# First loads, spectral norms, due steps and last outputs of a two-layer attention kernel

## The chip, the cores and the metric

The kernel runs on one core of a Trainium2 chip. A core has TensorE (PE, matrix products), VectorE (DVE), ScalarE (ACT), GpSimd (POOL) and SyncE (SP); each takes its instructions strictly in its own order, and they wait for each other by semaphores. Transfers between the memory and the core's buffers are issued by SP, ACT and POOL. The metric is the device time of one execution in microseconds (us), as the median of several runs. A profiled execution gives the busy times and waits below; its span runs from the first to the last instruction.

## The reference

The input x is 8 images of 64 x 64 pixels with 256 channels, in float32. Two layers follow each other.

Layer 0: `qkv = x @ w_qkv` gives queries and keys; the values are the keys. The first 128 channels attend in horizontal windows (8 rows of 64 pixels, 4 heads of 32 channels), the other 128 in vertical windows (8 columns). Beside this a depthwise 3x3 convolution runs over `hard_swish(v)`; then `context = hard_swish(attention + convolution)` and `x = context @ w_out + b_out`.

Layer 1: three small projections f, g, h (32 channels each) and one back to 256 channels, each weight divided by its spectral norm (`w / sigma`, one power step from a given vector u). All 4096 pixels of an image attend to all: `softmax(g f^T) h`, projected with `wv`, times gamma, plus x.

## The kernel before

Each image is a chain of units: 8 horizontal windows (h0 to h7, 4 steps each), 8 vertical windows (v0 to v7, 3 steps each) and 2 global units (l0, l1, 32 steps each); h0 of the next image stands ahead of l0. A step is a block of scores on TensorE (four heads as 32-row products, L777, L801, L1016), two exps on ScalarE into a ring of eight weight slots (L560), and a block of values products for the step before (L823, L830, L1032). VectorE adds up the weights for the softmax sums (L839, L847, L854, L1047); in the global units POOL's DMAs add up one of four head rows (L1056, L1058).

Everything else is a task that a planner, class `Flow`, fits between the steps while the program is built: projections of x in four quarters of two 256-column pieces (`project`, L306; m = 0 and 2 are the "near" queries and keys for the horizontal windows, m = 1 and 3 the "far" ones for the vertical windows), convolution taps (`conv`, eight on VectorE, L708), joins, clips and contexts, sums and norms, the layer-1 projections (`project_fg`, `project_h`), and the results (`result`). A task has a due step, made from the table `DUE` and the unit's own step, and pieces with estimated costs (`ADD`, `TAPS`, ...). `fill_pe`, `fill_act` and `fill_dve` take the ready task that is due first, as far as the planner's own clocks say that it fits; `require` runs a task at once when a step needs it. So a change of `DUE` or of a cost changes the order of instructions on every engine.

Ahead of the planned part, the program loads the weights (L351 to L392) and works out the spectral norms (L404 to L452): VectorE multiplies and reduces, three products on TensorE (L424, L425) sum over partitions, ScalarE takes a square root (L443). The first image's first load of x is issued on SP behind these loads (`load`, L617). A single bank of PSUM (`mm_tile`) serves projections, sums and norms in turn, so the next of them waits until the last is copied out. Keys reach the values products by a chain: eviction on ScalarE (L649), transpose on VectorE (L718), a DMA to memory (L723), four DMAs back (L734).

The end is written out by hand: `last_blocks` multiplies contexts by `w_out` and `last_ends` adds the global part (L1119), evicts with ScalarE (L1125) into two buffers `ot` and stores (L1129); `limits` checks the range of the softmax sums and sets a flag by a small product (L470). A flag out of range would start an exact second version of the kernel, which doesn't run with these inputs.

## Time and profile before

| | |
|---|---|
| median of 3 runs | 3292.57 us (3291.46 to 3293.92) |
| the profiled execution | 3294.1 us, span 3292.3 us |
| TensorE busy | 3244.5 us, 99% of the span |
| VectorE busy | 2666.3 us, 81% |
| ScalarE busy | 2667.3 us, 81% |
| GpSimd busy | 513.4 us, 16% |
| granted TensorE clock, mean | 0.996 |
| read from and written to HBM | 99.78 MB and 83.89 MB |

The profile names engines as PE (products), PEld (weight loads, which overlap PE), DVE, ACT, POOL and SP; PEq, ACTq and SPq are the sequencers that issue. L306 is line 306 of the kernel. In rows of groups and of the timeline, `out<-in` are the program's names of tiles, `32*128 32x512` the shape of weights and of what is streamed, `x8` how many instructions (one float32 product is two), and in brackets the idle time of the engine before them and what ended it. Matmuls are pipelined and their ends modelled, so start times tell more than ends.

### The profile page before, as it was taken

How to read it: one execution, taken by the hardware profiler on the slowest of the kernel's cores; microseconds unless marked ns; L12 is line 12 of the kernel's file. 1: busy time of each engine (PE TensorE's matmuls, PEld its weight loads, DVE VectorE, ACT ScalarE, POOL GpSimd, SP SyncE). 2: the span in 40 equal slices, each digit the busy share in tenths (PEclk: the TensorE clock that was granted, in tenths of full speed). 3: DMA queues.
4: the chain of work that ended last, by engine and by line, in shares of the span. 5: the costliest groups of instructions: out<-in, count | busy, mean ns of one | idle time of the engine just before them, and what ended most of it. 6: DMA issues, size and time to landing. Idle time of an engine off the chain costs nothing. (4 is left out here: it accounts for less than half of the span.)

```text
span 3292.3 us, 83473 instructions
## 1 busy us (share of the span) xinstructions
PE 3244.5 (99%) x35348; PEld 1191.2 (36%) x35348; DVE 2666.3 (81%) x2404; ACT 2667.3 (81%) x3235; POOL 513.4 (16%) x776
## 2 busy tenths in 40 slices
PE   7999999999999999999999999999999999999998
PEld 3344233432335323353233433334333443334422
DVE  4898688986989869897689976899768997789874
ACT  5778888887888878888788887888877888778785
POOL 0001320012200222002210032100321003210132
PEclk9999999999999999999999999999999999999999
DMA  2125653356433564335643365423753236632465
GB/s 73 58 85 118 126 105 100 88 116 132 105 92 91 114 134 97 94 95 115 132 97 91 95 126 125 97 86 98 135 120 98 81 106 127 125 94 69 108 123 108
DMA packets 321117, 344.40 MB, mean 105 GB/s; under 512 B 34272, under 2 KB 198624, under 8 KB 320736
## 3 DMA queue, kind: packets, MB, share of 16 engines
q0 software_dynamic: 71680, 134.25, 23.1%
q1 hardware_dynamic: 246816, 204.18, 21.0%
q8 instruction: 280, 4.59, 0.6%
q10 hardware_dynamic: 2240, 0.56, 0.1%
q14 instruction: 101, 0.83, 0.1%
HBM read 99.78 MB, written 83.89 MB: 56 GB/s over the span
## 5 line engine op out<-in xcount | busy, mean ns | idle before, releaser
L560 ACT ACTIVATE p<-s 128x1024 f32<-128x1024 f32 x1664 | 1612.2, 1024 | 195.3 <-PE s L1016 113.9
L1047 DVE TENSOR_TENSOR acc_l<-acc_l,p 128x1536 f32<-128x1536 f32 x480 | 842.7, 1756 | 312.1 <-ACT p L560 308.1
L708 DVE SCALAR_TENSOR_TENSOR act<-hv,dw_sb,act 128x1024 f32<-128x1024 f32 x512 | 653.5, 1280 | 15.2 <-ACT act L704 4.3
L1016 PE MATMUL s<-gq,f 32*128 32x512 f32 x4096 | 618.3, 641 | 1.7 <-DMA gq<-fg 1.7
L1032 PE MATMUL num_l<-p,h_sb 128*32 128x512 f32 x4096 | 545.4, 604 | 0.3 <-ACT nums_l L1062 0.3
L306 PE MATMUL pq<-x,wqkv_sb 128*32 128x256 f32 x8192 | 516.1, 381 | 4.4 <-ACT kv L653 2.1
L306 PEld LDWEIGHTS pq<-x,wqkv_sb 128*32 128x32 f32 x8192 | 265.2, 110 | 349.5 <-issue 191.3
L1016 PEld LDWEIGHTS s<-gq,f 32*128 32x128 f32 x4096 | 187.1, 183 | 332.4 <-issue 323.7
L801 PE MATMUL s<-qh,kh 32*128 32x512 f32 x2048 | 296.2, 640 | 6.5 <-ACT qh L634 5.7
L1058 POOL DMA_DIRECT2D row_l<-p x240 | 210.8, 878 | 522.5 <-ACT p L560 467.6
L1058 POOL DMA_DIRECT2D acc_l<-p x240 | 210.5, 877 | 426.7 <-ACT p L560 332.3
L830 PE MATMUL num_h<-p,vs 128*32 128x512 f32 x2048 | 272.8, 605 | 2.9 <-DMA vs<-kvia 2.7
L306 PE MATMUL s<-act,wout_sb 128*32 128x512 f32 x2048 | 227.6, 594 | 0.2 <-ACT ot_l L1125 0.2
L1032 PEld LDWEIGHTS num_l<-p,h_sb 128*32 128x32 f32 x4096 | 80.9, 108 | 383.8 <-issue 371.3
L777 PE MATMUL s<-qv,kv 32*128 32x256 f32 x3072 | 213.8, 394 | 1.4 <-ACT p L560 1.4
L1098 ACT ACTIVATE ot_l<-s,bias_o 128x512 f32<-128x512 f32 x120 | 76.0, 685 | 152.6 <-PE s L306 144.2
L823 PE MATMUL num_v<-p,vs 128*32 128x256 f32 x3072 | 193.6, 385 | 0.0
L839 DVE TENSOR_TENSOR acc_h<-p 128x2048 f32<-128x2048 f32 x64 | 146.3, 2285 | 53.5 <-PE sum_h L869 48.0
L1056 POOL DMA_DIRECT2D acc_l<-p x16 | 9.2, 577 | 1145.0 <-PE sum_h L869 961.5
L777 PEld LDWEIGHTS s<-qv,kv 32*128 32x128 f32 x3072 | 144.2, 184 | 78.4 <-issue 52.9
L839 DVE TENSOR_TENSOR acc_v<-p 128x2048 f32<-128x2048 f32 x64 | 146.6, 2291 | 21.0 <-PE sum_h L869 9.8
L790 ACT ACTIVATE p<-s 128x1024 f32<-128x1024 f32 x128 | 131.4, 1027 | 27.0 <-PE s L777 27.0
(140 smaller groups left out, 3214.6 us busy)
## 6 DMA issues: line engine op xcount, KB each, us to landing
acc_l<-p POOLq DMA_DIRECT2D x256, 256.0 KB, 3.3
row_l<-p POOLq DMA_DIRECT2D x256, 256.0 KB, 3.4
x<-in_xT SPq DMA_DIRECT2D x92, 512.0 KB, 4.1
kvia<-kt SPq DMA_DIRECT2D x128, 256.0 KB, 2.4
vs<-kvia SPq DMA_DIRECT2D x512, 64.0 KB, 2.1
out<-ot_l SPq DMA_DIRECT2D x128, 256.0 KB, 2.1
via_v<-nums_v SPq DMA_DIRECT2D x64, 256.0 KB, 2.1
shuf_v<-via_v SPq DMA_DIRECT2D x256, 64.0 KB, 2.1
```

What stands on the lines that cost most here:

```text
L306: nc.tensor.matmul(out[quad(r), :], lhsT=lhsT[:, quad(r)], rhs=rhs, start=start, stop=stop)
L560: nc.scalar.activation(pt[:, 2 * z : 2 * z + 2, :], sc[z], AF.Exp, scale=scale)
L708: nc.vector.scalar_tensor_tensor(o, src, wt, o, ALU.mult, ALU.add)
L777: mm = nc.tensor.matmul(place_of(n, r, h, sc), lhsT=k[quad(r), t * P : (t + 1) * P], rhs=q[quad(r), side(h)], start=True, stop=True,)
L801: nc.tensor.matmul(row_of(sc, r), lhsT=k[quad(r), c * P : (c + 1) * P], rhs=q[quad(r), :], start=True, stop=not exact,)
L823: nc.tensor.matmul(u["num"][quad(r), side(h)], lhsT=vs[kind, i][:, r, t, :], rhs=place_of(n, r, h, (pt[:, :2], u["mid", c], pt[:, 2:])), s ...
L830: nc.tensor.matmul(u["num"][quad(r), :], lhsT=vs[kind, i][:, r, c, :], rhs=u[c][:, r, :], start=(c == 0), stop=(c == 3),)
L839: nc.vector.tensor_add(u["acc"], u["acc"] if c == 2 else u[0], u[c])
L1016: nc.tensor.matmul(row_of(sc, r), lhsT=f4[quad(r), c * P : (c + 1) * P], rhs=gq[quad(r), z, :], start=True, stop=not exact,)
L1032: nc.tensor.matmul(u["num"][quad(r), :], lhsT=h_sb[:, c, :], rhs=u[c][:, r, :], start=(c == 0), stop=(c == 4 * NB - 1),)
L1047: nc.vector.tensor_add(acc, u[0][:, :rows, :] if c == 1 else acc, u[c][:, :rows, :])
L1058: nc.gpsimd.dma_start(out=u["row", c % 2], in_=u[c][:, rows, :], accum_op=ALU.add)
```

## The change

- The key half of `w_qkv` is loaded first on SP, then the first block of x, then the query half. `b_qkv` moves to ScalarE's queue; `dw`, `wv` (four copies), gamma and the small biases move from SP and ScalarE to POOL's queue.
- The spectral norms become four planner tasks (`scale`, `spread`, `norms`, `divide`) that run among the first image's steps, with their scratch in `f4`, which the first image needs only later. The square root is made on VectorE by four Newton rounds from an integer start value; ScalarE runs one dummy exp early.
- The planner charges 0.12 more for a VectorE task that depends on the one before it, with lower costs otherwise, and may take another ready task instead if that one's due step is at most `other` steps later (a value that can be negative).
- Due steps of their own for the first image (`first_...`), for each block's projections (`ahead`, `k`, `q`), swishes and joins, for the vertical windows' sums, release, norm and context, and for the results; all of the table has new values. Keys are required before queries at a window's start.
- The last unit's outputs go to eight slots of the weight ring in place of two buffers, and VectorE evicts every second of them; the last sums stand between two blocks of products.

Cut to its core, the diff is:

```diff
@@ DUE and costs
-    near_k=-7, near_q=-2, near_values=-50, clip=42, swish=21, conv_h0=106, conv_h1=18, conv_h2=27,
-    conv_h3=36, conv_v0=65, conv_v1=13, conv_v2=32, conv_v3=27, tap=-21, join_h=-53, join_hl=28,
-    join_v=12, context=-28, norm=14, release=-34, sums=-18, add=48, adds_h=1, adds_v=0, group_h=0,
-    group_v=1, add2=12, add3=98, apart=8, fg0=-7, fg2=-15, fg3=3, h0=36, h1=7, values_v=-102, near0=-69,
-    spread0=14, spread1=66, spread_mid=68, conv_first=80, far_swish=-20,
+    ahead1=104, ahead2=7, ahead3=1, ahead4=17, k0=-13, k1=52, k2=-18, k3=0, k4=-3, k5=18, k6=-3, k7=7,
+    q0=70, q1=31, q2=-14, q3=-2, q4=70, q5=4, q6=0, q7=99, join_h0=38, join_h1=17, join_h2=23,
+    join_h3=23, join_h4=-12, join_h5=26, join_h6=-17, join_h7=58, join_v0=26, join_v1=19, join_v2=20,
+    join_v3=-25, join_v4=-148, join_v5=-22, join_v6=22, join_v7=-5, swish1=98, swish2=-48, swish3=-133,
+    swish4=17, far_swish0=101, far_swish1=5, far_swish2=-23, far_swish3=28, far_swish4=46,
+    far_swish5=-127, far_swish6=3, far_swish7=-2, result0=121, result1=-27, release_v=-9, norm_v=11,
+    sums_v=-54, context_v=-34, clip_v=70, other=-91, first_ready=42, first_near=-1, first_k=1,
+    first_q=-2, first_swish_v=-3, first_swish_h=54, first_conv_h=6, first_conv_v=22, near_k=-4,
+    near_q=91, near_values=-10, clip=141, swish=12, conv_h0=168, conv_h1=16, conv_h2=24, conv_h3=39,
+    conv_v0=17, conv_v1=23, conv_v2=29, conv_v3=69, tap=-21, join_h=-73, join_hl=24, join_v=1,
+    context=-43, norm=18, release=-7, sums=66, add=26, adds_h=1, adds_v=0, group_h=0, group_v=1,
+    add2=-44, add3=93, apart=6, fg0=-7, fg2=31, fg3=120, h0=32, h1=12, values_v=-74, near0=-55,
+    spread0=4, spread1=72, spread_mid=61, conv_first=309, far_swish=-2,
 )
...
-ADD, ADD3, NORM, SWISH, TAP, TAPS = 2.36, 1.83, 2.5, 0.75, 0.75, 1.28
+ADD, ADD3, NORM, SWISH, TAP, TAPS, BOUND = 2.21, 1.68, 2.39, 0.61, 0.61, 1.2, 0.12
...
@@ Flow
+                if engine == "dve":
+                    took += BOUND * self.bound(task)
+                    self.dve_last = task
...
+    def bound(self, task):
+
+        return task is self.dve_last or self.dve_last in task.needs
+
...
-                self.run(min(ready, key=lambda k: k.due))
+                best = min(ready, key=lambda k: k.due)
+                if self.bound(best):
+                    others = [k for k in ready if not self.bound(k) and k.due <= best.due + DUE["other"]]
+                    best = min(others, key=lambda k: k.due, default=best)
+                self.run(best)
...
@@ first loads
+    three_e = const.tile([P, 1], F32, name="three_e")
 
     wqkv_sb = const.tile([P, 2, 2 * C], F32, name="wqkv_sb")
-    nc.sync.dma_start(out=wqkv_sb, in_=w_qkv.rearrange("(k p) m -> p k m", p=P))
+    wq = w_qkv.rearrange("(k p) m -> p k m", p=P)
+    nc.sync.dma_start(out=wqkv_sb[:, :, C:], in_=wq[:, :, C:])
+    later = [lambda: nc.sync.dma_start(out=wqkv_sb[:, :, :C], in_=wq[:, :, :C])]
     bqkv_sb = const.tile([P, 4], F32, name="bqkv_sb")
-    nc.sync.dma_start(out=bqkv_sb, in_=b_qkv)
+    nc.scalar.dma_start(out=bqkv_sb, in_=b_qkv)
     h_sb = const.tile([P, N // P, D], F32, name="h_sb")
     raw = h_sb[:, : 2 * 3, :].rearrange("p (k z) d -> p k z d", k=2)
...
-    u_r = rows(ufgh.rearrange("z o d -> o (z d)"), 3 * D, "u_r")
-    wv_raw = prep.tile([P, C], F32, name="wv_raw")
-    for r in range(NQ):
-        nc.sync.dma_start(out=wv_raw[quad(r), :], in_=wv)
-    uv_r = rows(uv, C, "uv_r")
-    gam = rows(gamma, 1, "gam")
...
-    pb = mm_tile("norms")
-    for k in range(2):
-        nc.tensor.matmul(pb[:, :NF], lhsT=ones, rhs=ext[:, k, :], start=(k == 0), stop=(k == 1))
-    nc.tensor.matmul(
-        pb[:, NF : NF + C + 1], lhsT=ones[:D, :], rhs=ext_v[:D, :], start=True, stop=True
-    )
-    sums = prep.tile([P, NF + C + 1], F32, name="sums")
...
-    nc.scalar.activation(inv, inv, AF.Sqrt)
...
+    def spectral(scratch):
...
+        u_r = rows(ufgh.rearrange("z o d -> o (z d)"), 3 * D, nc.scalar)
+        uv_r = rows(uv, C, nc.scalar)
+        nc.scalar.dma_start(out=wout_sb, in_=w_out.rearrange("(k p) m -> p k m", p=P))
+        nc.gpsimd.dma_start(out=dw_sb, in_=dw)
+        nc.gpsimd.dma_start(out=dwb_sb, in_=dw_bias)
+        wv_raw = part(C)
+        for r in range(NQ):
+            nc.gpsimd.dma_start(out=wv_raw[quad(r), :], in_=wv)
+        gam = rows(gamma, 1, nc.gpsimd)
+        nc.gpsimd.dma_start(out=bout_c, in_=b_out)
+        nc.gpsimd.dma_start(out=b_raw, in_=bfgh)
+        bv_c = part(2)
+        nc.gpsimd.dma_start(out=bv_c, in_=bv)
...
+        def scale():
+            nc.vector.tensor_scalar_mul(wout_sb, wout_sb, 1.0 / 6.0)
+            nc.vector.tensor_scalar_mul(dw_sb, dw_sb, 1.0 / 6.0)
+
+        def spread():
...
+        def norms():
+            pb = mm_tile("norms")
+            for k in range(2):
+                nc.tensor.matmul(
+                    pb[:, :NF], lhsT=ones, rhs=ext[:, k, :], start=(k == 0), stop=(k == 1)
+                )
+            nc.tensor.matmul(
+                pb[:, NF : NF + C + 1], lhsT=ones[:D, :], rhs=ext_v[:D, :], start=True, stop=True
+            )
+            nc.vector.tensor_copy(sums, pb[:, : NF + C + 1])
+        def divide():
...
+            nc.vector.tensor_scalar(
+                root.bitcast(I32), inv.bitcast(I32), -0.5, float(0x5F3759DF), ALU.mult, ALU.add
+            )
+            for _ in range(4):
+                nc.vector.tensor_mul(t, root, root)
+                nc.vector.tensor_mul(t, t, inv)
+                nc.vector.tensor_scalar(t, t, -0.5, 1.5, ALU.mult, ALU.add)
+                nc.vector.tensor_mul(root, root, t)
+            nc.vector.tensor_mul(inv, inv, root)
...
+        return scale, spread, norms, divide
...
@@ load
+                while later:
+                    later.pop()()
...
@@ last_blocks, last_ends
-                    if js[0] == 0:
-                        u["po", m] = []
-                    pair = pairs.popleft()
-                    pairs.append(pair)
-                    for i, j in enumerate(js):
-                        u["po", m].append(pair[:, i, :])
+                    for j in js:
+                        if j % 2 == 0:
+                            pair = pairs.popleft()
+                            pairs.append(pair)
+                            u["po", m] = [*u.get(("po", m), ()), pair[:, 0, :], pair[:, 1, :]]
...
-                        ot = work.tile([P, TB], F32, tag="ot", name=f"ot_{nm}_{j}_{m}", bufs=out_bufs)
-                        nc.scalar.activation(
-                            ot, u["po", m][j], AF.Identity, bias=bias_o[:, m : m + 1]
-                        )
+                        ot = weights_at(4 * m + j, 1)[:, 0, :]
+                        if j % 2:
+                            nc.vector.tensor_scalar_add(ot, u["po", m][j], bias_o[:, m : m + 1])
+                        else:
+                            nc.scalar.activation(
+                                ot, u["po", m][j], AF.Identity, bias=bias_o[:, m : m + 1]
+                            )
...
@@ the norms as tasks
-        combined = []
+        combined, scaled = [], []
         if not exact:
+            scale, spread, norms, divide = spectral(f4)
+            nc.scalar.activation(three_e, three, AF.Exp)
+            scaled.append(flow.add("dve", [(scale, [("dve", NORM)])], 6, ready=1))
+            k = flow.add("dve", [(spread, [("dve", NORM)])], 7, ready=1)
+            k = flow.add("pe", [(norms, [("pe", 1.5), ("dve", TAP)])], 10, [k], ready=3, bank=True)
+            k = flow.add("dve", [(divide, [("dve", 5.5)])], 14, [k], ready=4)
             combined.append(
-                flow.add("pe", [(combined_weights, [("pe", 5.0), ("dve", NORM)])], 24, ready=16, bank=True)
+                flow.add(
+                    "pe", [(combined_weights, [("pe", 5.0), ("dve", NORM)])], 24, [k, *scaled], ready=16,
+                    bank=True,
+                )
             )
...
@@ due steps
+                total.then = (last, e + DUE["sums" if u.kind != "v" else "sums_v"])
...
+            u.released = flow.add("act", [(u.release, [("act", COPY)])], e + DUE["release" if u.kind != "v" else "release_v"], ready=e)
...
+                due = start + inside_due(i, 0) + DUE[f"ahead{i}"] if inside else None
...
+                    ready, due = (start, start + inside_due(i, 1) + DUE[f"{'kq'[m == 1]}{i}"]) if last else (0, u.t + DUE["first_k" if m == 3 else "first_q"])
...
+                        due = start + inside_due(i, 1) + DUE["far_swish"] + DUE[f"far_swish{i}"] if last else u.t + DUE["first_swish_v"]
...
+                        due += 0 if last else DUE["first_conv_v" if half else "first_conv_h"]
...
+                    due += DUE[f"join_{'hv'[kind]}{i}"]
...
-                    u.ends.append(flow.add("res", pieces, u.t + u.steps + 4 * m, [u.normed], im.ends[-1:]))
+                    u.ends.append(flow.add("res", pieces, u.t + u.steps + DUE[f"result{m}"], [u.normed], im.ends[-1:]))
-                h[i].ahead = {0: [near[i, 0], near[i, 2]]}
+                h[i].ahead = {0: [near[i, 2], near[i, 0]]}
...
...
@@ the end
-                u.last_blocks(0, (2, 3))
+                u.last_blocks(0, (2,))
                 flow.require(u.total, u.released)
+                u.last_blocks(0, (3,))
                 u.last_blocks(1, (0, 1))
                 flow.require(u.normed)
```

## The prediction

> **What bounds the kernel now.** I read the page first: TensorE is busy for 99% of the span, VectorE and ScalarE for 81% each.
>
> ```profile
> PE 3244.5 (99%) x35348; PEld 1191.2 (36%) x35348; DVE 2666.3 (81%) x2404; ACT 2667.3 (81%) x3235; POOL 513.4 (16%) x776
> PE   7999999999999999999999999999999999999998
> ```
>
> So only what makes TensorE wait, or stretches a row of it, can be won. Second, the busy times by stretch (columns: stretch and length, then busy time and instructions of PE, PEld, DVE, ACT, POOL, then clock, DMA share, GB/s): the first 40 us, a slow stretch, the vertical windows of the second image, and the end.
>
> ```profile
> 0.00:20.00 20.00, 7.80 (x70) 3.75 (x70) 6.48 (x27) 2.68 (x4) 1.59 (x16) 1.00 0.33 87
> 26.70:33.40 6.70, 5.79 (x44) 2.56 (x48) 2.89 (x2) 1.54 (x3) 0.00 (x0) 0.50 0.02 5
> 585.00:684.00 99.00, 99.00 (x1340) 48.84 (x1340) 91.85 (x97) 85.69 (x105) 0.00 (x0) 1.00 0.31 89
> 3258.00:3292.00 34.00, 21.72 (x180) 6.03 (x176) 7.64 (x15) 8.86 (x13) 1.74 (x2) 0.87 0.31 88
> ```
>
> TensorE does nothing useful for 12.2 of the first 20 us and 12.3 of the last 34; from 26.7 to 33.4 its clock is half; and in the vertical windows VectorE is at 93%, next in line to bound.
>
> Third, the timeline, which shows what a step costs. First the global stage without a filler, then a step with one quarter of a projection.
>
> ```profile
> 721.72 1.31 PE L1016 MATMUL s<-gq,f 32*128 32x512 f32 x8
> 723.96 1.14 PE L1016 MATMUL s<-gq,f 32*128 32x512 f32 x8
> 726.02 1.34 PE L1016 MATMUL s<-gq,f 32*128 32x512 f32 x8
> ...
> 803.68 1.14 PE L1016 MATMUL s<-gq,f 32*128 32x512 f32 x8
> 805.63 0.61 PE L306 MATMUL pq<-x,wqkv_sb 128*32 128x256 f32 x8
> 806.18 1.14 PE L1016 MATMUL s<-gq,f 32*128 32x512 f32 x8
> ```
>
> Starts of scores: plain steps take 2.24 and 2.06 in turn (the odd one waits for an exp to free a bank), the one with a quarter 2.50. Sorting all 512 global steps of the trace by content: plain 2.154 on average with 2.066 the least, one quarter 2.50, two 2.93, four 3.79, that is 2.066 + 0.43 per quarter. A filled step hides what the exps cost; a plain one after a plain one loses.
>
> Last, timeline and chain rows at the start, at the last image's global stage, and at the end.
>
> ```profile
> 7.11 0.40 SPq L617 DMA_DIRECT2D x<-in_xT  x1
> 13.17 3.51 PE L306 MATMUL pq<-x,wqkv_sb 128*32 128x256 f32 x32 [0.71 <-DVE sums L429]
> 27.61 1.94 PE L830 MATMUL num_h<-p,vs 128*32 128x512 f32 x8 [2.66 <-DMA vs<-kvia]
> 178.79 1.07 PE L830 MATMUL num_v<-p,vs 128*32 128x512 f32 x8 [3.12 <-DMA vs<-kvia]
> 190.11 1.07 PE L869 MATMUL sum_v<-acc_v,ones 128*32 128x256 f32 x16 [1.79 <-DVE acc_v L854]
> 3092.07 2.04 PE L1016 MATMUL s<-gq,f 32*128 32x512 f32 x2 [1.73 <-DMA gq<-fg]
> 3281.76 1.28 ACT L1125 ACTIVATE ot_l<-s,bias_o 128x512 f32<-128x512 f32 x2 [2.68 <-PEq L1562]
> 3285.39 1.28 ACT L1125 ACTIVATE ot_l<-s,bias_o 128x512 f32<-128x512 f32 x2 [2.35 <-DMA out<-ot_l]
> ```
>
> The first projection starts at 13.17, behind the norms on TensorE; each of the next four rows is a wait of TensorE; the last evictions wait for output buffers.
>
> **The change part by part.** Gains are against the profiled execution: 3294.1, of which 3292.3 is span; it lies 1.5 above the median 3292.57, so I take the same gain off the median.
>
> *Start.* The first image load moves from seventh to second on SP's queue: SP's second issue stood at 1.26, so it leaves 5.85 earlier than 7.11. The page's median landing of such a load is 4.1, which gives 5.4; wqkv's halves land beside it, so I take 6.2. The norms no longer stand ahead on TensorE, so the first projection gains 13.17 - 6.2 = 7.0. Bounds: 7.8 (landing as the median); 4.0 if 1.0 MB must pass first at the 131 GB/s of the best 100 us (7.9 us, start at 9.2). The wv, gamma and bias loads go to POOL's queue, ten issues at about 0.88 (the POOL rows), all out before 11, and the halo memsets behind them aren't needed until about 20. ScalarE keeps seven issues and loads the exp table before there is anything to evict; the two loads of 1.28 (at 9.57 and 21.45) become one.
>
> *First values.* Keys are projected before queries. From the end of the key eviction to the first values product the trace has 20.19 to 27.61, 7.4. In the new order TensorE fills this with 0.05 + query projection 1.93 + 0.82 to its eviction's end, scores 1.07, projection 1.75, scores 0.95 = 6.6, so about 0.8 of the 2.66 stays: 1.9 won. The clock fell to 0.50 from 26.7 to 33.5 after this gap, 6.8 us at half, 3.4 lost; gaps of 0.8 elsewhere leave it at 1.00, so I count the 3.4 too: 5.3 (1.9 to 6.0). The next image load now waits on SP behind the value fetches (issue near 16, landed near 20.5; its projection comes near 22.5).
>
> *First image's h windows.* Before, steps with waits lose 0.27, 0.88, four times 1.61, 1.65, 1.73 and 1.20 = 12.2. In the new order each of seven windows starts with far-query projection, values, near-query projection, scores: 0.81 for the query's eviction (the trace's wait) and about 0.1 for the bank (two evictions of 0.42 beside values of 0.95), and the norms' step puts two projections back to back, 1.0 more: 7.4. I take 4 of the 4.8; bounds 0 (ScalarE isn't free and each is 1.6 again) and 6. The norms' VectorE work (3.7 to spread, some 34 small rows at 0.16 to 0.2 to divide, four Newton rounds among them) falls before about 55, where VectorE is under half busy; if it were not hidden it would cost up to 8.
>
> *First image's v windows.* The last far projection stands a scores, values and projection (3.6) earlier: covers the 3.12. The first sums stand a step (2.9) later: covers 1.79. A ring-slot wait (1.18) and 3.4 us of half clock at 204.2 (1.7) follow VectorE's backlog, which I leave: 5. Bounds 0 and 8.
>
> *Due steps.* Counted in the order of both programs: plain global steps in images 1 to 7 fall from 171 to 15 (in the last from 57 to 51), steps with one quarter rise from 87 to 247, with a whole projection fall from 77 to 21. 156 x 0.088 = 13.7. Before the first global block's sums two evictions (0.71 each) delay the exp, 1.07 per image; now one stands there: about 0.35 saved in each of six, 2. So 16. Bounds: 0 (evictions in more steps delay exps by as much) and 26 (the waits near 0.3 that VectorE causes in the v windows, some 2 per image, go too). The rule in `fill_dve` chooses nothing: a task due 91 before the one due first doesn't exist. Only its costs count.
>
> *Last image.* The wait at 3092.07 with the half clock after it costs 6.0 over two steps. The second fg projection now stands before its values (1.3) and its fetches ahead of a shuffle that held SP's queue for 2.60: 3.9, over the wait. 6; bounds 2.5 and 6.9.
>
> *End.* Eight ring slots in place of two buffers, half the evictions on VectorE. TensorE's last product ends at 3279.9. New is that the flag's product stands on TensorE behind VectorE's two evictions (about 0.65 each, by the copy from PSUM of 0.52 for 356 columns): it goes at about 3275.85 instead of 3273.77, the last 32 products at 3276.5 instead of 3275.20, so TensorE ends at 3281.2, the evictions at 3282.1 rather than 3286.67, less 0.4 for a second issue: 4. Bounds 1 and 5.9.
>
> Sum: 7.0 + 5.3 + 4 + 5 + 16 + 6 + 4 = 47.3; 3292.57 - 47.3 = 3245.3.
>
> [...] In the rows above, a step with a quarter is longer by its own 0.43 and nothing else, and the count of changes between 32-row and 128-row products is 2004 in both orders. [...]
>
> The trace's clock fell after a 2.66 gap and stayed at 1.00 after one of 3.12. [...]
>
> **The rivals.**
>
> A, only the ends gain. Quarters bring as many eviction delays as they hide, and the first image's windows keep their waits: 7.0 + 5.3 + 6 + 4 = 22.3, 3270. For it: ScalarE is at 82% in the global stage (161.65 of 197). Against: a quarter leaves 0.4 spare per step.
>
> B, VectorE's waits go too, as the due steps of joins and contexts move: the bounds 26, 8 and 6 in the sum, 62, 3231. For it: VectorE work from the first v add to the first global one falls from 102.8 to 95.2 by counts times rows.
>
> C, slower: VectorE becomes the bound in the h windows. From h1's first add to v0's it gets 30 taps instead of 26, 105.5 us of work instead of 99.5, while TensorE's own work there is 106.9. From 1.4 us on, each further us delays TensorE as at 190.11. To eat 47 over seven images it must be late by 6.7 in each, five taps beyond the margin: 3300 with a little more.
>
> D, planner changes that move little but the start: 3285.
>
> **How the numbers follow.** Forecast 0.60, A 0.19, B 0.11, C 0.06, D 0.04. The range runs from near B to below D: 3224 to 3279, about 0.83. A measurement here tells 0.2% (6.6 us) from nothing: faster 0.93, same 0.01, slower 0.06. The likeliest's own range is 3230 to 3260.
>
> **What would show it.** Right: first projection near 6; no half clock before 34; plain global steps near 66 and TensorE's waits of 1.79 and 3.12 gone; the time between the same step of successive images, 403.2 in this trace, shorter by about 2.3; evictions at the end without waits for output DMAs, and one new wait of the flag's product for VectorE. Wrong: spread's rows blocking VectorE behind late POOL loads, rows of the exp waiting for VectorE's adds in the h windows, or a period of 403 or more.

## The result and the profile after

The changed kernel takes 3265.53 us as the median of four runs (3263.12 to 3267.18), the kernel before 3292.02 beside it: a ratio of 0.9918 with a 95% interval of 0.9901 to 0.9935, so some 27 us faster. The forecast was 3245 with a range of 3224 to 3279: the sign and the range hold, the size does not (47 was expected), and 3265.5 is outside the likeliest case's own range.

The profiled execution takes 3267.18, its span 3265.4. First the page's busy times and TensorE's slices of the changed kernel:

```profile
PE 3218.2 (99%) x35348; PEld 1166.6 (36%) x35348; DVE 2659.7 (81%) x2426; ACT 2653.4 (81%) x3230; POOL 516.4 (16%) x786
PE   8999999999999999999999999999999999999998
```

Both kernels run 35348 products; the 26.3 us that TensorE is less busy are rows that take less time. Then the same stretches as before: the first 20 us, the second image's vertical windows, the last 34 us.

```profile
0.00:20.00 20.00, 12.78 (x132) 5.24 (x136) 3.58 (x12) 6.99 (x10) 7.01 (x26) 1.00 0.48 140
567.60:667.10 99.50, 99.49 (x1344) 48.50 (x1340) 92.92 (x102) 86.73 (x106) 0.00 (x0) 1.00 0.32 89
3231.00:3265.00 34.00, 22.89 (x176) 6.20 (x172) 10.13 (x18) 5.79 (x9) 1.77 (x2) 0.88 0.32 89
```

The start gives TensorE 5.0 more; the vertical windows are as tight as they were, with VectorE at 93% still; the last 34 us hardly gain. The clock column reads 1.00 for the first 20 us because the trace's clock record begins only with the first rise, at 14.31 here; what runs at half clock before it is seen from the lengths of the rows: in the trace of before, a projection takes 3.67 where the record reads 0.50 (at 29.29) and 1.93 where it reads 1.00 (at 17.50). The timeline of the start shows what was won and what was not:

```profile
1.26 0.46 SPq L663 DMA_DIRECT2D x<-in_xT  x1
5.61 3.64 PE L326 MATMUL pq<-x,wqkv_sb 128*32 128x256 f32 x32 [5.61 <-DMA x<-in_xT]
10.05 3.64 PE L326 MATMUL pq<-x,wqkv_sb 128*32 128x256 f32 x32 [0.80 <-ACT kh L697]
14.50 1.14 PE L849 MATMUL s<-qh,kh 32*128 32x512 f32 x8 [0.81 <-ACT qh L682]
18.51 1.07 PE L878 MATMUL num_h<-p,vs 128*32 128x512 f32 x8
```

The first projection stands at 5.61 instead of 13.17, but the second one, which took 1.93 before, now takes 3.64: it too runs at half clock. The first values stand at 18.51 with no wait at all, and nothing is slow behind them.

In the following, step n is the n-th block of scores in the written order (0 to 959; steps 0 to 31 are the first image's horizontal windows, 32 to 55 its vertical ones; an image has 120). The gain up to a step is its start in the one trace less its start in the other, corrected by TensorE work that the new order carries across it, at the 0.86 that 2048 columns of products take (two quarters of a projection: steps of 2.93 against 2.07). The terms of the forecast's sum against it:

| term | steps | forecast | measured |
|---|---|---|---|
| start | to 0 | 7.0 | 5.5 |
| first values | 0 to 2 | 5.3 | 5.9 |
| first image's h windows | 2 to 32 | 4 | 1.0 |
| first image's v windows | 32 to 60 | 5 | 4.1 |
| rest of the first image | 60 to 124 | 0 | 0.9 |
| due steps, images 2 to 7 | 124 to 844 | 16 | 4.8 |
| last image | 844 to 959 | 6 | 5.1 |
| end | from 959 | 4 | -0.6 |
| sum | | 47.3 | 26.7 |

Two terms, the due steps and the end, are 16 of the 20 that are missing. The due steps' 4.8 are themselves a difference: in images 2 to 7 the vertical windows gain 1.7 and the global stage with the next image's first window 19.6, more than was forecast, and the horizontal windows lose 16.5. In the global stage of the changed kernel, a timeline in image 2 shows the step with one quarter of a projection at 2.50, as it was:

```profile
778.90 0.61 PE L326 MATMUL pq<-x,wqkv_sb 128*32 128x256 f32 x8
779.45 1.14 PE L1064 MATMUL s<-gq,f 32*128 32x512 f32 x8
781.94 1.14 PE L1064 MATMUL s<-gq,f 32*128 32x512 f32 x8
784.44 1.14 PE L1064 MATMUL s<-gq,f 32*128 32x512 f32 x8
```

Where the horizontal windows lose is seen at the last of them in image 2, in the changed kernel's timeline:

```profile
552.74 0.61 PE L326 MATMUL pq<-x,wqkv_sb 128*32 128x256 f32 x8
553.47 1.04 SPq L663 DMA_DIRECT2D x<-in_xT  x2
554.59 1.14 PE L849 MATMUL s<-qh,kh 32*128 32x512 f32 x8 [1.24 <-ACT qh L682]
557.63 1.93 PE L326 MATMUL pq<-x,wqkv_sb 128*32 128x256 f32 x32 [0.91 <-DMA x<-in_xT]
```

and in the list of TensorE's waits over the whole span (us in total, times, longest):

```profile
PE s L849 <- ACT qh L682: 13.9, 14, 1.2
PE pq L326 <- DMA x<-in_xT: 10.6, 7, 5.6
PE good L516 <- DVE lim L514: 2.6, 1, 2.6
```

The query projection of block 7 ends with the quarter at 552.74, right before the scores that need it: 1.24 for its eviction. Then comes the near query projection of the next image's block 0. It is due 91 steps behind its window now (`near_q`), so it stands behind the second load of block 0, which is made for the far projections; the program's table `xt` then names that load's tile, and the product waits for it: 0.91. The keys of the same block, seven steps earlier, read the first load. Of the 10.6 for x, 5.6 is the start; 5.0 falls on these places of six images. Neither wait was in the trace of before.

Last the end, in the timeline:

```profile
3247.11 1.41 DVE L1173 TENSOR_SCALAR p<-s,bias_o 128x512 f32<-128x512 f32 x2 [3.07 <-ACT p L1175]
3248.98 0.19 PE L516 MATMUL good<-lim,ones 128*1 128x2 f32 x2 [2.63 <-DVE lim L514]
3250.16 5.30 PE L326 MATMUL s<-act,wout_sb 128*32 128x512 f32 x32
3256.57 0.69 ACT L1175 ACTIVATE p<-s,bias_o 128x512 f32<-128x512 f32 x1 [5.61 <-PE s L1166]
3257.29 0.75 DVE L1173 TENSOR_SCALAR p<-s,bias_o 128x512 f32<-128x512 f32 x1 [5.54 <-ACT p L1175]
```

No eviction waits for an output transfer any more. But the flag's product waits 2.63 behind VectorE's evictions, the 32 products behind it take 5.30 instead of 3.64, and each of VectorE's evictions starts only when ScalarE's has ended.

### The profile page after: what moved, and what is told of

The parts are those of the page before. It is cut to its first block, busy times and chain, and to the rows that moved or that the text cites. A ratio compares the mean times of both kernels' runs of the same rounds, so it can differ in the third digit from the quotient of the medians.

```text
span 3265.4 us, 83524 instructions
## 1 busy us (share of the span) xinstructions
PE 3218.2 (99%) x35348; PEld 1166.6 (36%) x35348; DVE 2659.7 (81%) x2426; ACT 2653.4 (81%) x3230; POOL 516.4 (16%) x786
## 4 chain that ended last, share of the span: by engine, by line
PE 84%; DVE 9%; ACT 3%; DMA 2%; issue 1%; SPq 0%; DVEq 0%; ACTq 0%
PE s L1064 17%; PE num_l L1080 15%; PE pq L326 12%; PE s L849 8%; PE s L326 7%; PE num_h L878 6%; PE s L825 4%; PE num_v L871 4%; PE sum_v L917 3%; DVE act L756 3%; PE sum_h L917 3%; PE pf L987 1%; DVE acc_v L887 1%; PE num_v L878 1%; ACT p L606 1%
## 5 line engine op out<-in xcount | busy, mean ns | idle before, releaser
L756 DVE SCALAR_TENSOR_TENSOR act<-hv,dw_sb,act 128x1024 f32<-128x1024 f32 x512 | 654.0, 1278 | 25.9 <-ACT act L752 16.5
L1064 PE MATMUL s<-gq,f 32*128 32x512 f32 x4096 | 594.1, 640 | 1.1 <-ACT ot_l L1146 1.1
L326 PE MATMUL pq<-x,wqkv_sb 128*32 128x256 f32 x8192 | 547.1, 381 | 14.0 <-DMA x<-in_xT 10.6
L1064 PEld LDWEIGHTS s<-gq,f 32*128 32x128 f32 x4096 | 168.7, 182 | 260.7 <-issue 247.1
L895 DVE TENSOR_TENSOR acc_h<-acc_h,p 128x2048 f32<-128x2048 f32 x64 | 146.1, 2282 | 7.8 <-ACT p L606 7.1
```

The source lines that it names most:

```text
L326: nc.tensor.matmul(out[quad(r), :], lhsT=lhsT[:, quad(r)], rhs=rhs, start=start, stop=stop)
L756: nc.vector.scalar_tensor_tensor(o, src, wt, o, ALU.mult, ALU.add)
L1064: nc.tensor.matmul(row_of(sc, r), lhsT=f4[quad(r), c * P : (c + 1) * P], rhs=gq[quad(r), z, :], start=True, stop=not exact,)
```

## The experiments

All are compared with the kernel before on the same chip; ratios are given with their 95% intervals. The changed kernel's own is 0.9918 (0.9901 to 0.9935).

### The late queries: block 0 alone, all blocks, and both waits

Theory: the late query projections are where the steady gain went. Rival: the waits only show that another engine is late, and would turn up a step further on. The first edit takes block 0's query out of its late place.

```
-  (u.t + DUE["near_k" if m else "near_q"] + ...
+  (u.t + ((91 if i else -2) if last and not m else DUE["near_k" if m else "near_q"]) + ...
```

> The changed kernel with one due step different: in images 2 to 8 the near query projection of block 0 alone is due 2 steps before its window instead of 91 behind it; the rest of the order moves only as the planner follows. In the changed kernel that projection stands behind the second load of block 0 and reads that load's tile: TensorE waits 0.91 at 557.63 for it, and the scores before it wait 1.24 for the query of block 7. Theory 1 (the late queries are where the steady gain of the due steps went): the wait for x goes in six images, the one for the query stays, 0.9 x 6 = 5.5, so 3260 (3257 to 3262), and the time between equal steps of successive images falls from about 402.0 to 401. Theory 2 (TensorE's waits there only stand for VectorE's or ScalarE's lateness, which shows up a step later): 3264 to 3267.

Measured: 3272.29, ratio 0.9937 (0.9924 to 0.9951), some 6 us slower than the changed kernel, which neither theory gave. TensorE's waits in its profile:

```profile
PE s L849 <- ACT qh L682: 11.3, 14, 0.8
PE pq L326 <- ACT qh L682: 7.4, 6, 1.2
PE pq L326 <- DMA x<-in_xT: 6.3, 1, 6.3
```

The wait for x is gone in all six images (the 6.3 is the start). In its place the planner put block 0's query right ahead of block 7's, and since one bank of PSUM serves both, the second waits 1.23 for the first one's eviction and then delays its own scores by 0.81: 7.4 in the place of 5.0. The 1.24, which stood in seven images, became 0.81. Against the changed kernel's trace, images 2 to 7 lose 1.0 each up to these two projections, win 0.2 to 0.9 in the four steps behind them and lose another 0.6 to 0.9 in the vertical windows; what the last is due to was not followed up.

The second edit moves the queries of all blocks of images 2 to 8 outside the global stage (-2 instead of 91).

> The changed kernel with the near query projections of all blocks of images 2 to 8 outside the global stage due 2 steps before their windows instead of 91 behind. Theory 1: both waits of the h windows, 0.91 for x and 1.24 for the query, go and nothing comes in their place: (0.9 + 1.3) x 6 or 7 = 13 to 15, so 3251 (3249 to 3256). Theory 2 (the cause is elsewhere): 3264 to 3267. Theory 3: the planner's other steps, which were set with the late queries, fit no longer, sums of the v windows are cut into more pieces, and what the queries win is lost in the v windows: 3258 to 3270.

Measured: 3390.64, ratio 1.0300 (1.0286 to 1.0314): 125 slower, beyond every theory. What the trace shows fits the mechanism of theory 3, far larger than was thought. The list of waits has

```profile
PE s L825 <- ACT p L606: 41.5, 83, 4.6
PE pq L326 <- DMA x<-in_xT: 15.6, 7, 5.7
```

the vertical windows' scores wait 83 times for an exp, the six waits for x even grow (9.9 without the start's 5.7), and the trace loses 12 to 17 in every image from the second on, 13.8 of it in the second image's vertical windows. TensorE's sums of these windows, which stand in 64 steps in the changed kernel's trace, are cut over 117 here. The first of these rows is a third of the 125; the rest was not taken apart. A due step can't be judged by the task that it belongs to.

So the third edit was chosen by its written order: due steps for block 0's keys and query and block 7's query were varied until nothing else moved. In images 2 and 3 six steps of 120 differ.

```
+  (u.t + ((-30 if m else -20) if n > 1 and not i else -1 if last and i == 7 and not m
+          else DUE["near_k" if m else "near_q"]) + ...
```

> The changed kernel with three due steps different in images 2 to 8: near projections of block 0 of images 3 to 8 at 30 (keys) and 20 steps (queries) before its window, the near query projection of block 7 one step before its window. In images 2 and 3 the order of TensorE then differs in six steps of the h windows alone and in nothing else: keys of block 0 in steps 141 and 142 of the program, the query of block 7 in 143, the query of block 0 in 145 and 146, so that none stands against another's eviction (what the run with block 0's query alone did wrong: 7.4 of waits for ScalarE came in place of 5.0 for x) and none behind the second load of block 0. Theory 1: both waits, 5.0 for x in six images and 1.2 for the query in seven, go and nothing comes in their place: 13, so 3252 (3250 to 3256), and 2.1 less from image to image. Theory 2 (another engine is as late, and the waits only show it): 3262 to 3267.

Measured: 3252.14, ratio 0.9875 (0.9860 to 0.9890), 13.4 faster than the changed kernel where 13 was expected. Its list of waits:

```profile
PE s L849 <- ACT qh L682: 6.5, 8, 0.8
PE pq L326 <- DMA x<-in_xT: 5.7, 1, 5.7
```

Both waits are gone but for one place, and nothing came instead; the time between equal steps of successive images is 399.3 to 399.8 in images 2 to 6, against 401.3 to 402.7 in the changed kernel and 403.2 in the one before. The rival falls: these 13 us of the forecast's missing 20 were lost at the places to which `near_q` had put these two queries.

### All due steps taken back

> The changed kernel with every due step and every cost of the kernel before (the new names at values that change nothing): new loads, norms, keys first, the end in ring slots stay. The forecast's sum has 16 for the due steps and some 5 of the first image's windows: 3265.5 + 21 = 3286. The trace of the changed kernel, which shows about 4.6 won over images 2 to 7, 4 in the first image's v windows and 4 to 6 in the last image, says 3277 (3273 to 3281). A rival in which only the new start and end brought anything says 3266 to 3268.

The edit gives the changed kernel the old table and the old costs:

```
-DUE = dict(ahead1=104, ..., far_swish=-2)
-ADD, ADD3, NORM, SWISH, TAP, TAPS, BOUND = 2.21, 1.68, 2.39, 0.61, 0.61, 1.2, 0.12
+DUE = dict(<the old values; new names at values that change nothing>)
+ADD, ADD3, NORM, SWISH, TAP, TAPS, BOUND = 2.36, 1.83, 2.5, 0.75, 0.75, 1.28, 0.0
```

Measured: 3305.82, ratio 1.0037 (1.0023 to 1.0051). All three expectations miss: without its due steps the change is a loss of 13. By the trace this kernel stands 11.3 ahead of the one before at step 4, 9.5 behind it at step 60, and from there to the last step keeps that distance to within about 2. Its timeline shows the longest of the first image's waits:

```profile
100.62 7.83 DVE L744 SCALAR_TENSOR_TENSOR act<-hv,dw_sb,act 128x1024 f32<-128x1024 f32 x6
108.48 0.69 DVE L946 TENSOR_TENSOR act<-nums_h,act 128x512 f32<-128x512 f32 x1
109.96 0.69 DVE L955 SCALAR_TENSOR_TENSOR act<-nums_h,act 128x512 f32<-128x512 f32 x1 [0.79 <-ACT nums_h L950]
110.69 0.59 ACT L917 COPY nums_h<-num_h 128x512 f32<-128x512 f32 x1 [0.76 <-DVE act L955]
111.33 1.93 PE L866 MATMUL num_h<-p,vs 128*32 128x512 f32 x8 [4.28 <-ACT nums_h L917]
113.03 3.60 PE L314 MATMUL pq<-x,wqkv_sb 128*32 128x256 f32 x32
```

Read upwards: TensorE's values wait 4.28 for a numerator to be copied out, that copy for a buffer of the window four before, that for its context, the context for its join, the join for six taps of the convolution on VectorE. And the clock halves behind it. Between 95 and 215 us this trace has 11.8 of such waits for numerators and values, and from 109 to 247 its granted clock is 0.50 for 20.5 us, half of which is lost. The taps are late. The next three runs ask why.

### Why the first image lost: three theories, two of them wrong

First theory: the norms' rows on VectorE stand in the taps' way. The rows are left out, the order kept:

```
 def spread():
-    nc.vector.tensor_mul(ext[:, :, : 3 * D], flat, ...)
-    ...
+    pass
```

> The kernel with the old due steps and the new start (3305.8), with all rows of the spectral norms on VectorE and TensorE left out, two that scale wv and add the bias kept; the order of all else is the same. The outputs are therefore those of unnormalised weights: the run measures time alone. Left out are some 9 us of small rows on VectorE before 105 us. Theory 1 (with the new start these rows stand where VectorE has the first image's taps to do; the contexts come late, numerators wait for a free buffer, 4.28 at 111.33, the clock halves behind each such wait): most of the 22 us that this kernel loses to the one before between steps 20 and 60 comes back, 3287 (3283 to 3293). Theory 2 (the old due steps do not fit keys first and loads early, whatever the norms do): 3300 to 3306.

Measured: 3302.12, ratio 1.0027 (1.0016 to 1.0038): theory 1 falls. The same waits are there, in the same places.

Second theory: it is not the rows but the time that the planner reserves for them. Their planned costs become zero.

```
-  k = flow.add("dve", [(divide, [("dve", 5.5)])], 14, [k], ready=4)
+  k = flow.add("dve", [(divide, [("dve", 0.0)])], 14, [k], ready=4)
```

> The kernel of the old due steps without the norms' rows (3302.1) with their planned times set to zero as well, so that the planner places the first image's taps as if nothing of the norms were there; outputs of unnormalised weights again. Ahead of the sums of window h4 the written order then has 16 taps, where the kernel before has 13 to 22, the old due steps with the new start 9. Theory 1 (the planner reserves some 11 us of VectorE for the norms in the first windows and so writes the taps a window too late, whether or not the time is used; contexts, numerators and TensorE wait on them): the loss of 22 against the kernel before in the first image goes and the start's 11 stay, 3283 (3279 to 3292). Theory 2 (keys first and the early loads, not the norms, spoil the old due steps): 3298 to 3306.

Measured: 3310.16, ratio 1.0056 (1.0043 to 1.0070). This theory falls too, and with it the reading that the number of taps ahead of a window decides: this order has more of them early. One numerator now waits 12.2, again at the end of the same chain, behind eight taps in a row:

```profile
150.24 10.60 DVE L693 SCALAR_TENSOR_TENSOR act<-hv,dw_sb,act 128x1024 f32<-128x1024 f32 x8 [3.33 <-ACT act L689]
163.72 1.93 PE L815 MATMUL num_h<-p,vs 128*32 128x512 f32 x8 [12.19 <-ACT nums_h L866]
```

Third theory: the old due steps fit the one plan for which they were set, and another input to the planner gives a worse one. For this the kernel before, with its own start, its norms and all its instructions, gets three empty tasks:

```
+  k = flow.add("dve", [(lambda: None, [("dve", NORM)])], 7, ready=1)
+  k = flow.add("pe", [(lambda: None, [("pe", 1.5), ("dve", TAP)])], 10, [k], ready=3, bank=True)
+  k = flow.add("dve", [(lambda: None, [("dve", 5.5)])], 14, [k], ready=4)
```

> The kernel before with three tasks that do nothing given to the planner (2.5 and 5.5 us of VectorE, 1.5 of TensorE, as the new norms' tasks cost): loads, norms and all instructions stay, only the written order of the first image follows another plan. Built, it has ahead of the sums of windows h3, h4 and h5 5, 9 and 17 taps, as the old due steps with the new start have, where the kernel before has 9, 13 and 26. Theory 1 (the old due steps fit the one plan that they were set for, and any other input of the planner writes a worse first image): the 22 that the old due steps lost there, without the start's 11: 3314 (3307 to 3319). Theory 2 (the old due steps fail with the new start because work of the start stands in the first image's way on the engines, and the order as such is harmless): 3291 to 3297.

Measured: 3317.17, ratio 1.0072 (1.0059 to 1.0086), 25.6 slower than the kernel before with nothing but its order changed. Its trace loses 23.1 from step 4 to step 60, as the old due steps with the new start lost 20.9 there, and the same row is back:

```profile
124.69 1.94 PE L830 MATMUL num_h<-p,vs 128*32 128x512 f32 x8 [4.27 <-ACT nums_h L881]
```

So the new tasks alone are enough to spoil the plan of the old due steps, whatever they do on the chip. They are not the only thing that does: the run before had them at a planned time of zero and lost 27.9 in the same steps. Which other part of the change does it, their place in the order, keys first or the loads, was not tried. Of the 40.3 that the new due steps are worth on top of the new start and end (3305.82 - 3265.53), the traces put 26 between steps 4 and 60, some 7 between there and the last image's global stage and 5.7 into that stage's first steps; the 26 repair what the other edits do to the plan. Which single due step repairs it was not tried.

### The norms in the changed kernel

The same rows are left out of the changed kernel, with its due steps.

> The changed kernel, due steps as they are, with the same rows of the spectral norms left out (outputs of unnormalised weights; time alone is measured). The forecast held these rows hidden, with up to 8 if they are not. Theory 1 (hidden, since the new due steps start the taps earlier): 3264 to 3265.5, less the 1.0 of the norms' step on TensorE. Theory 2 (they still push VectorE's backlog into the first image's v windows): 3259 to 3262.

Measured: 3260.65, ratio 0.9904 (0.9889 to 0.9919), which overlaps the changed kernel's interval. The number alone lies in the second theory's range; the traces decide against that theory. By them, 1.05 of it is the norms' step on TensorE, between steps 8 and 12. Between steps 12 and 92, where VectorE's backlog would show, the gain stays at 1.9, so the norms' rows on VectorE are hidden. The rest lies in the clock of the first 15 us and in later images; there the profile of the next run, whose order is the changed kernel's up to the end, gains 3.8 on it as well, so that is what one execution differs from another by. Part of it is the wait for x (3.3 to 5.0 in five profiles of this order).

### The end: old, and with the flag moved

The old way to evict is put back (`ot` buffers, all eight on ScalarE):

```
-  ot = weights_at(4 * m + j, 1)[:, 0, :]
-  if j % 2:
-      nc.vector.tensor_scalar_add(ot, u["po", m][j], bias_o[:, m : m + 1])
-  else: ...
+  ot = work.tile([P, TB], F32, tag="ot", ...)
+  nc.scalar.activation(ot, u["po", m][j], AF.Identity, bias=bias_o[:, m : m + 1])
```

> The changed kernel with the end of the kernel before in part: the last eight evictions all on ScalarE, into two buffers that wait for output transfers. Forecast's term: the new end is worth 4 (1 to 5.9), so 3269.5. By the changed kernel's trace, where the program ends 7.4 after the last eviction instead of 5.6 and the product for the flag waits 2.63, the new end is worth nothing: 3265 to 3267.

Measured: 3264.15, ratio 0.9913 (0.9898 to 0.9928): not to be told from the changed kernel. From step 959 to the end of the span its trace has 34.5, the changed kernel's 35.1, the kernel's before 34.6. Part of these lengths has nothing to do with the edit: from the end of the last eviction to the end of the span it is 5.6 to 7.4 in the profiles (5.67 in the kernel before and in the run with the old due steps, which has the new end; 7.37 in the changed kernel; 6.91 here). Up to the last eviction the three have 27.6, 27.8 and 28.9. The new end is worth nothing beside the old way to evict.

Then the four small rows that the flag's product reads go ahead of the evictions on VectorE:

```
-  u.last_ends(0, range(NQ)); limits()
+  limits()            # reductions and comparisons of the sums' range
+  u.last_ends(0, range(NQ))
+  limits_end()        # the product, and the flag
```

> The changed kernel with the four small rows on VectorE that the flag's product reads put before the last evictions, so that this product stands behind nothing. Theory 1 (the product's wait of 2.63 for VectorE and the half clock behind it, 1.7, are what ate the gain of the end): a wait of about 1 for a bank stays, TensorE ends some 3.3 to 4.3 earlier, 3261.8 (3261 to 3263). Theory 2 (the eight output transfers set the end, so that an earlier TensorE ends no earlier program): 3264.5 to 3266.

Measured: 3260.48, ratio 0.9901 (0.9886 to 0.9916). The intervals overlap, and the number is 0.5 below the first theory's range; the trace is clearer, with 31.1 from step 959 to the end, 4.1 less, and 23.9 to the last eviction, 3.9 less:

```profile
3244.55 0.19 PE L518 MATMUL good<-lim,ones 128*1 128x2 f32 x2
3246.18 3.64 PE L326 MATMUL s<-act,wout_sb 128*32 128x512 f32 x32 [0.38 <-DVE p L1175]
3251.64 0.75 DVE L1175 TENSOR_SCALAR p<-s,bias_o 128x512 f32<-128x512 f32 x1 [3.97 <-ACT p L1177]
```

The product waits for nothing, the 32 products take 3.64, and the end follows TensorE: theory 1 holds, and the output transfers don't set the end. VectorE's eviction still waits for ScalarE's.

### The clock at the start, and all together

Five products that nobody reads stand ahead of the first projection:

```
+  warm = mm_tile("warm")
+  for _ in range(5):
+      nc.tensor.matmul(warm[:, :P], lhsT=ident, rhs=ones, start=True, stop=True)
```

> The changed kernel with five products of 128 by 128 of the two constant tiles on TensorE before its first projection, in the time in which it waits for the image (about 1.5 to 5.6), their output read by nobody. In the profiles so far the first projection stands at 5.6 to 6.3 and takes 3.64 instead of 1.93, and the clock comes up at about 9.5, 13.8 or 18, differing between runs of one order; the first values stand at 17.5 to 20.8. Theory 1 (what the clock counts is TensorE's activity, so that earlier activity raises it earlier): second projection at 1.93 in every run, first scores at 11 to 12.9 instead of 14.5, the step behind the first values 0.9 to 3 earlier: 3262 to 3264.5. Theory 2 (it comes up at its own times, or the values' fetches are next in line at 17.5 and take all of it): 3265 to 3267.

Measured: 3261.75, ratio 0.9906 (0.9891 to 0.9921): a little under the first theory's number, with an interval that overlaps the changed kernel's, so the number decides nothing. In its profiled run these products didn't bring the clock up: they ran from 1.46 to 3.96, and the projection at 16.88 still takes 2.85, the next one 1.91:

```profile
1.46 2.50 PE L1213 MATMUL warm<-ones,ident 128*128 128x128 f32 x10 [1.46 <-POOL three L373]
10.41 3.64 PE L326 MATMUL pq<-x,wqkv_sb 128*32 128x256 f32 x32 [0.80 <-ACT kh L697]
16.88 2.85 PE L326 MATMUL pq<-x,wqkv_sb 128*32 128x256 f32 x32
```

That neither shows nor refutes activity as the cause: TensorE is idle for 2.01 behind them in this profile, and products without such a gap were not tried. Last, the parts together, with the evictions divided by pairs of banks (`if j >= 2` in place of `if j % 2`):

> The changed kernel with the due steps of the run without both waits (3252.1), the flag's rows ahead of the evictions (5.0 in its own run), the evictions divided by pair of PSUM banks (0 and 1 of each half on ScalarE, 2 and 3 on VectorE) so that VectorE's do not wait for ScalarE's, and the five products ahead of the first projection. If the parts add up: 3252.1 - 4 for the flag - 0.7 for VectorE's last eviction, which started 0.7 behind ScalarE's, - 1 to 2 for the clock: 3246 (3243 to 3249). If the end is set by the output transfers: 3249 to 3252.

Measured: 3246.09 (3244.79 to 3248.62), ratio 0.9864 (0.9849 to 0.9879), faster than both kernels, and the expected sum of its parts. VectorE's first pair of evictions starts with ScalarE's instead of behind it, but the last pair then stands on VectorE alone, one behind the other. From step 959 to the end of the span it has 30.2, 0.9 less than with the flag alone; up to the last eviction only 0.3 less (23.6), so the 0.7 expected of the pairs is not shown. Of the 1 to 2 for the clock, this profile has 1.5 at step 0 (12.98 against the changed kernel's 14.50): its second projection takes 1.93, as it does in two profiles without the five products.

```profile
3228.97 2.46 ACT L1177 ACTIVATE p<-s,bias_o 128x512 f32<-128x512 f32 x4 [5.14 <-PE s L1168]
3229.03 1.41 DVE L1175 TENSOR_SCALAR p<-s,bias_o 128x512 f32<-128x512 f32 x2 [2.03 <-PE s L1168]
3230.28 3.64 PE L326 MATMUL s<-act,wout_sb 128*32 128x512 f32 x32 [0.17 <-ACT p L1177]
```

## Why the prediction was right in sign and too large

*Start*, 7.0 forecast, 5.5 measured. The first projection gained 7.56, a little more than was thought, since x landed 4.35 after its issue. The mis-sized part is the second projection, silently taken at its old 1.93: it takes 3.64 here. That is not the order's doing alone: in the profile of the kernel before with three empty tasks, whose first instructions are those of the kernel before, the second projection takes 3.64 too, and in the three profiles of the new start whose clock rose by 10 us the start gained 7.1 to 7.3. So in this term the forecast is off by no more than one execution differs from another.

*First values*, 5.3 and 5.9. The wait went altogether rather than to 0.8, because the projection at half clock gave the fetches 1.7 more. Where the clock rose by 10 us, a wait of 0.54 to 0.83 does remain. No half clock followed. Right, and slightly small.

*First image's h windows*, 4 and 1.0. The bound of 0 was written for the reason that took it: ScalarE isn't free, and the window starts cost 1.2 to 1.6 each instead of 0.9. The norms' step costs the 1.0 that was put down for it, and the norms on VectorE are hidden, as was said.

*First image's v windows*, 5 and 4.1. Both waits, 3.12 and 1.79, are gone.

But these two terms stood on a wrong base. The forecast read them as what the new order wins over the old one and left the old order in place as the alternative. The runs show that the old due steps don't survive the other edits: with the new tasks in the planner the first image loses 21 to 23 from step 4 to step 60. That there was a net 5 in the first image's windows is 26 won against 21 lost.

*Due steps*, 16 and 4.8. The count was sound: 66 plain global steps remain, as said, and the stage won 19.6 over six images, more than the 16: the step with the first global block's sums fell from 4.86 to 3.78 in images 2 to 7, so the whole 1.07 of the two evictions went in each, where 0.35 was put down. What failed is a term that the sum doesn't have, the horizontal windows of images 2 to 7, put at nothing without a reason; they lost 16.5. The forecast sorted the global steps by content, but of these windows it only weighed VectorE's load (rival C). It did not read what stands where in them: a query projection next to the scores that need it, and a projection behind a load that renames its tile. Those two waits cost 13.4, by the run without them; its trace still loses 4.8 in these windows, which stays unexplained. With them gone, the period is 3.4 to 3.9 shorter than before in images 2 to 6, more than the 2.3 forecast. The statement that the new rule in `fill_dve` chooses nothing follows from the code: the task due first is the least of those ready, so none is due 91 steps before it.

*Last image*, 6 and 5.1: the wait of 1.73 for gq and the half clock behind it are gone, as said.

*End*, 4 and -0.6. The new wait was foreseen, with its place and its cause, and the term was mis-sized in three places. The wait was put at 2.1 and took 2.63. No loss of clock was counted behind it, while the forecast itself had counted 3.4 for one behind the wait of 2.66 at the start: 1.66 (5.30 for 3.64). VectorE's evictions were taken to run beside ScalarE's; they run behind them, 0.72 at the last. A further 1.7 of the difference isn't the change's: it lies behind the last eviction, where profiles with the same end differ as much. Up to the last eviction the changed kernel gained 1.1 (28.9 to 27.8). The run with the flag moved wins the wait and the half clock back (3.9 up to the last eviction); the evictions in pairs show no more than 0.3.

The clock behind a wait: by a row of before the forecast counted a loss behind the wait of 2.66, and in the changed kernel's profile a wait of 2.63 brings half clock too (0.50 from 3250.15 to 3253.56). But the length of the gap alone doesn't decide. The same wait of 2.63 for the flag stands in nine of the profiles: in seven the 32 products behind it take 5.30 to 5.91, in two (block 0's query alone, and the norms unplanned) they take 3.64.

Rival A, at 3270 the nearest in number, is not what happened: quarters did win their stage, and only the windows of the other stage kept the gain. That 3265.5 lies in the stated range is owed to these rivals, which stretched it upwards to 3279, and not to the sum. B and D did not happen. C, VectorE as the bound in the h windows, did not either: the stage did lose, for another reason.

## What to carry to other kernels

When a planner writes the order, an edit's cost can't be summed from the edit: three tasks that do nothing cost this kernel 25.6 us. So measure the new tasks with the old settings before crediting the new settings, and read the stages that the change is not about. For each moved product ask what its operand's name means at the new place, who has the accumulator bank before it, and what needs its result next. And a small product that reads another engine's result belongs ahead of that engine's long rows, or TensorE pays for the wait, 2.63 here, and, in seven of nine profiles here, for half clock behind it.

## What the runs showed of the hardware

The clock's rise at the start differs between runs of practically the same first instructions, by far more than the start itself does. In the profiles of the ten kernels with the new start and nothing ahead of it, the first projection stands at 5.6 to 6.3. In one of them (the norms left out of the changed kernel) the first projection takes 3.37 and the second 1.93. In one (without both waits) the second takes 1.93, from 10.19 on. In five both take 3.64, and the first scores, at 14.5 to 14.9, take 1.14. In three both take 3.64 as well, the scores 2.09, and the projection behind them, at 16.6 to 17.2, still 2.62 to 2.86, where it takes 1.93 in the others. From the timeline of the run without both waits:

```profile
10.19 1.93 PE L326 MATMUL pq<-x,wqkv_sb 128*32 128x256 f32 x32 [0.80 <-ACT kh L697]
```

and of the run with the flag moved, whose order is the same up to there:

```profile
10.18 3.64 PE L326 MATMUL pq<-x,wqkv_sb 128*32 128x256 f32 x32 [0.80 <-ACT kh L699]
16.64 2.80 PE L326 MATMUL pq<-x,wqkv_sb 128*32 128x256 f32 x32
```

The first projection began within 0.01 of the same time in both (5.75 and 5.74), and the step behind the first scores stands at 15.87 in the one and 19.38 in the other: 3.5 us from nothing in the program. The first values' fetches take back 0.6 to 0.9 of an early rise: in the two profiles whose second projection takes 1.93, the values wait 0.54 and 0.83 for them.

The clock records of two traces show when the granted clock changed. In the kernel before it rises at 16.41, 3.24 behind the start of the first projection, and is 0.50 from 26.66 to 33.48, from 204.15 to 207.56, from 3091.82 to 3098.65 and from 3282.97 on. In the changed kernel it rises at 14.31, 8.70 behind the start of the first projection and with 0.80 idle between the first two, and is 0.50 from 3250.15 to 3253.56 and from 3260.39 on. In both, changes that are close in time lie 3.41, 6.82, 6.83 or 10.25 us apart, one to three times 3.41. What sets the rise is not shown: no run varied the gap of 0.80.

What decides a fall stays open too: the kernel before kept the clock through the wait of 3.12 ahead of 178.79 and lost it at 204.15, behind waits of 1.18 and 0.20 (at 202.66 and 203.58).

Two evictions from one pair of PSUM banks on two engines ran one behind the other, 0.72 apart, though they read different banks (ScalarE's at 3250.28, VectorE's at 3251.00 in the changed kernel); in different pairs they ran together (3228.97 and 3229.03 in the run of all parts). In the built program VectorE's eviction waits for ScalarE's in the one case and for TensorE's product in the other, so it is the built program that puts them in a row.
